# A sparse graph transformer on one core: key products in place, three product buffers, two blocks of states kept in SBUF, output scatters moved and joined

## The chip, the cores and the metric

The kernel runs on one core of a Trainium2 chip. The metric is device time in microseconds (us) of one execution, all four layers included. The engines are named as in the profile: PE (TensorE matmul) and PEld (its weight loads), DVE (VectorE), ACT (ScalarE), POOL (GpSimd) and SP (SyncE, which here only issues transfers).

## The reference

Input `x` holds 16 graphs of 1024 nodes with 128 features, all graphs over the same adjacency matrix `adj` (1024x1024, each entry 1 with probability 1/128). Four layers follow each other: attention, graph attention, attention, attention.

```
def attention_layer(adj, h, ...):            # layers 0, 2, 3
    Q, K, V = h @ Wq, h @ Wk, h @ Wv         # 8 heads of 16
    scores = einsum('bnhd,bmhd->bhnm', Q, K) / sqrt(16)
    scores = where(adj == 0, -inf, scores)
    o = einsum('bhnm,bmhd->bnhd', softmax(scores), V)
    x = layer_norm(h + (o @ Wo + bo), ln1_g, ln1_b)
    y = relu(x @ W1 + b1) @ W2 + b2          # 128 -> 256 -> 128
    return layer_norm(x + y, ln2_g, ln2_b)

def graph_attention_layer(x, adj, ...):      # layer 1
    h = x @ W
    e = leaky_relu((h @ a_src)[:, :, None] + (h @ a_dst)[:, None, :], 0.2)
    att = nan_to_num(softmax(where(adj == 0, -inf, e)))
    return layer_norm(att @ h + x)           # with gain and shift
```

## The kernel before

The function `sparse_path` uses the sparsity of the matrix. Only neighbours enter a softmax, so the kernel gathers the rows of each node's neighbours instead of forming 1024x1024 scores. A second function, `dense_path`, stands behind a flag for inputs that the sparse form can't take; it isn't run here.

**Tiling.** The 16 graphs form two groups (`g`, GR = 2) of eight. The 1024 nodes, reordered by degree, form eight blocks (`t`, T = 8) of 128. A *unit* is one (layer, g, t); `units` lists all 64, and the program goes through them in that order. A unit's state tile, `xs[l, g, t]`, is 128 x (2 halves x 4 graphs x 128) float32, which is 512 KB; the halves `h` go through the tails one by one.

**Tables and gathers.** When a unit of layer l is finished, `project` (L573) writes its new state into the DRAM buffer `kept` (L576, 256 KB for each half) and the projected keys and values into the DRAM table of layer l+1 (L593). All table rows of a group must have been written before that group of the next layer begins. For a unit of the next layer, `loaded` (L881) fetches the state back into a tile of the pool `inputs` (L901, 512 KB), two units ahead; in layer 0 it gathers it from the input (L889). `gathered` (L956) issues indirect transfers from POOL's queue (L971), each bringing one table row to each of the 128 partitions: in an attention layer a row has eight graphs' keys (ROW = 1024 numbers) and values (another 1024), 8 KB. Rows of empty slots are skipped.

**Parts.** A unit's gathered rows are worked off in *parts*, held in `parts`. In an attention layer a unit has five: four with two chunks of rows, and, in fourth place, one shared chunk (`MIX`) of left-over rows. A graph attention unit has three parts, of four, three and two chunks. `es[i]` is the gather buffer of part i; there are four (`EDGES`), so a gather for part i+3 is issued after the last use of part i-1.

**The loop** (L1235) takes one part an iteration. `begun` is the iteration in which the current unit began. In iteration i:

- `products(i)` (L979, L985): DVE multiplies gathered keys with queries into a tile of the pool `prods` (tag `pr`, 8 KB a partition, four buffers). For the shared part POOL does this, in `product_of_shared` (L1000), issued two iterations earlier.
- `summed(i - 2)` (L1067, L1062): PE adds up the weighted values of an earlier part over its rows into `acc`. In attention it takes the first two parts of a unit together. This is what releases a `pr` tile.
- `exponentials(i)` (L1009): DVE sums the products over each head (L1018), ACT takes the exponential (L1022).
- `weighted(i - 1, 0)` (L1036, L1046): DVE multiplies values with the exponentials into the same `pr` tile; in graph attention, which has no key products, the tile is allocated here, and a second call `weighted(i - 1, 2)` takes the part's other two chunks.
- then POOL's work, in this order (L1287): the gathers of part i+3, the shared part's product of part i+2 if that is one, and any output scatter that is in the list `ready`.
- `others()`, three or four times an iteration: steps of the *tails*.

In iteration begun+1 the previous unit is divided by its denominators (L1099, L1102), and its two tails, one for each half, start (`attention_tail` L714, `graph_tail` L766). A tail is a generator: each `yield` is a place where the loop may go on with something else. `PLANS` says by hand which half's tail or which query step runs at each `others()`. The tail of unit u runs while unit u+1 is worked off, and ends in `finish` (L671). In layers 0 to 2 `finish` transposes the state into a tile of the pool `states` and calls `project`. In layer 3 it transposes it back into the tile `outs` (L689) and scatters it to the output rows with an indirect transfer from POOL: a unit's scatter (L702, both halves, 512 KB) goes into `ready`, and only the last unit scatters each half by itself as soon as it is there (L695, 256 KB each, with the row numbers in `halves`). With the plan of layer 3 a unit's `outs` is complete in iteration begun+1 of the unit after the next, so its scatter is issued there, behind the two gathers of part begun+4 and L1000. All scatters write the tensor `out`, and each waits for the one before it to land.

The line that decides on what is issued between gathers:

```
gathered(i - 1 + AHEAD)
product_of_shared(i + 2)
while ready:
    ready.pop(0)()
```

Of the kernel before, what the change touches and what calls it, by code (L numbers as in the profile page):

```python
# [14 lines left out]
F32 = mybir.dt.float32  # L15
# [7 lines left out]
P = 128  # L23
# [21 lines left out]
GR = 2  # L45
# [18 lines left out]
)  # L64
TOP = -(-max(map(max, CAPS)) // 8) * 8
QUADS = TOP // S
MIX = J


# [75 lines left out]
def sparse_path(ctx: ExitStack, tc: tile.TileContext, a: dict, out: bass.AP, flag):  # L145
# [46 lines left out]
    marks = const.tile([P, len(MARK), 32], F32, name="marks")  # L192
    nc.gpsimd.memset(marks, 0.0)
    places = const.tile([P, GR, T], I32, name="places")
    halves = const.tile([P, HF], I32, name="halves")
    bad = const.tile([P, T], F32, name="bad")
    seen = const.tile([P, 2, G * H], F32, name="seen")
    nc.gpsimd.memset(seen, 0.0)
# [37 lines left out]
    def graph(wide):  # L236
# [152 lines left out]
        for g in range(GR):  # L389
            nc.vector.tensor_scalar(  # L390
                places[:, g, :], there, float(GR), float(g), ALU.mult, ALU.add,
            )
        for h in range(HF):
            nc.vector.tensor_scalar(
                halves[:, h : h + 1], there[:, T - 1 :], float(GR * HF), float((GR - 1) * HF + h),
                ALU.mult, ALU.add,
            )
        low = s1.tile([P, T], F32, name="low")
        nc.vector.tensor_tensor(bad, sorted_[:, :, 2], caps[:, :T], ALU.is_gt)
        nc.vector.tensor_scalar(low, sorted_[:, :, 2], 1.0, None, ALU.is_lt)  # L400
# [166 lines left out]
        for l in range(1, len(LAYERS)) for g in range(GR)  # L567
    }
    xs = {}
    srcs = {}  # L570


    def project(l, g, t, h, x, kv=None):  # L573

        if l:
            nc.sync.dma_start(kept[l, g][t, :, h, :], x.rearrange("p g n -> p (g n)"))  # L576
        table = tables[l, g][t * P : (t + 1) * P, :]
        if LAYERS[l][1] is ATTN:
            if kv is None:
                kv = twos.tile([P, 2, GH, D], F32, tag="kv", name="kv")  # L580
            for i in range(0, GH, 2):
                ps = bank([P, 2, 2 * D])
                for k in range(2):
                    nc.tensor.matmul(  # L584
                        ps[:, k, :], x[:, i + k, :], w[LAYERS[l][0], "Wkv"],
                        start=True, stop=True,
                    )
                nc.scalar.copy(  # L588
                    kv[:, :, i : i + 2, :].rearrange("p c g d -> p g c d"),
                    ps.rearrange("p g (c d) -> p g c d", d=D),  # L590
                )
                yield
            nc.sync.dma_start(  # L593
                table.rearrange("p (c x) -> p c x", c=2)[:, :, h * GH * D : (h + 1) * GH * D],
                kv.rearrange("p c g d -> p c (g d)"),
            )
            return
        kv = twos.tile([P, GH * D + GH], F32, tag="kv", name="kv")
        if h == 0:
            srcs[g, t] = const.tile([P, G], F32, name=f"src{g}{t}")  # L600
        for i in range(0, GH, 2):
            ps = bank([P, 2, D + 2])
            for k in range(2):
                nc.tensor.matmul(ps[:, k, :], x[:, i + k, :], wg, start=True, stop=True)
            nc.scalar.copy(
                kv[:, i * D : (i + 2) * D].rearrange("p (g d) -> p g d", d=D), ps[:, :, :D]
            )
            to = GH * D + i
            nc.scalar.copy(
                kv[:, to : to + 2].rearrange("p (g o) -> p g o", o=1), ps[:, :, D : D + 1]  # L610
            )
            at = h * GH + i
            nc.scalar.copy(
                srcs[g, t][:, at : at + 2].rearrange("p (g o) -> p g o", o=1), ps[:, :, D + 1 :]
            )
            yield

        nc.sync.dma_start(table[:, h * GH * D : (h + 1) * GH * D], kv[:, : GH * D])
        nc.sync.dma_start(table[:, ROW + h * GH : ROW + (h + 1) * GH], kv[:, GH * D :])
# [51 lines left out]
    def finish(l, g, t, h, z, gain, shift, dve=False):  # L671
        if l + 1 < len(LAYERS):

            wanted[0] = True
            while held[0]:
                advance(slow)
            wanted[0] = False
            busy[0] += 1
            xn = states.tile([P, GH, P], F32, tag="xT", name="xT")
            turned(z, xn, gain, shift)  # L680
            yield "free"
            yield from project(l + 1, g, t, h, xn)
            busy[0] -= 1
            return
        xn = states.tile([P, GH, P], F32, tag="xT", name="xT")
        turned(z, xn, gain, shift, dve)
        yield
        if h == 0:
            leaving[g, t] = twos.tile([P, HF, GH, D], F32, tag="kv", name="outs")  # L689
        o = leaving[g, t]  # L690
        turned(xn, o[:, h], dve=dve)
        yield
        yield
        if (l, g, t) == units[-1]:
            nc.gpsimd.indirect_dma_start(  # L695
                out=out.rearrange("n (k c) -> (n k) c", k=GR * HF),
                out_offset=bass.IndirectOffsetOnAxis(ap=halves[:, h : h + 1], axis=0),
                in_=o[:, h].rearrange("p g d -> p (g d)"), in_offset=None,
            )
        elif h + 1 == HF:  # L700
            rows = o.rearrange("p h g d -> p (h g d)")
            ready.append(lambda: nc.gpsimd.indirect_dma_start(  # L702
                out=out.rearrange("n (k c) -> (n k) c", k=GR),
                out_offset=bass.IndirectOffsetOnAxis(ap=places[:, g, t : t + 1], axis=0),
                in_=rows, in_offset=None,
            ))

    def hidden():
        return ones_.tile([P, F * GH * P], F32, tag="f1", name="f1")
# [171 lines left out]
    def loaded(u):  # L881
# [1 line left out]
        if u >= len(units):  # L883
            return
        l, g, t = units[u]
        xs[units[u]] = inputs.tile([P, HF, GH, P], F32, tag="x", name="x")
        if l == 0:
            x = xs[units[u]]
            nc.gpsimd.indirect_dma_start(  # L889
# [89 lines left out]
    def products(i):  # L979
        u, (piece,) = parts[i]  # L980
        if i in prs:
            return
        n = len(piece)
        prs[i] = [prods.tile([P, 2, ROW], F32, tag="pr", name="pr")]
        nc.vector.tensor_tensor(  # L985
            prs[i][0][:, :n, :], es[i][:, :n, :ROW],
            of_piece(qs[u], piece),
            ALU.mult,
        )

    def product_of_shared(i):

# [43 lines left out]
    def weighted(i, k0):  # L1036

        u = parts[i][0]
        ex, n = exs_of(i)
        if n <= k0:  # L1040
            return
        m = min(2, n - k0)
        base, d = (ROW, HD) if is_attention(u) else (0, D)
        if not is_attention(u):
            prs.setdefault(i, []).append(prods.tile([P, 2, ROW], F32, tag="pr", name="pr"))
        nc.vector.tensor_tensor(  # L1046
            prs[i][k0 // 2][:, :m, :].rearrange("p k (a d) -> p k a d", d=d),
            es[i][:, k0 : k0 + m, base : base + ROW].rearrange("p k (a d) -> p k a d", d=d),
            ex[:, k0 : k0 + m, :]
            .rearrange("p k (a o) -> p k a o", o=1)  # L1050
            .to_broadcast([P, m, ROW // d, d]),
            ALU.mult,
        )
# [135 lines left out]
    with tc.manual_schedule():  # L1189
# [33 lines left out]
                        advance(slow)  # L1223
                        break
        scratch.close()
        prods = ctx.enter_context(tc.tile_pool(name="prods", bufs=4))
        smalls = ctx.enter_context(tc.tile_pool(name="smalls", bufs=3))
        nc.gpsimd.memset(wide[3], 0.0)
        gathered(AHEAD - 1)
# [5 lines left out]
        for i in range(len(parts) + 2):  # L1235
# [46 lines left out]
            if 0 < i <= len(parts):  # L1282
# [3 lines left out]
                    weighted(i - 1, 2)  # L1286
                gathered(i - 1 + AHEAD)  # L1287
                product_of_shared(i + 2)
                while ready:
                    ready.pop(0)()  # L1290
                for _ in sizes:
                    pass
# [472 lines left out]
```

## Time and profile before

| | |
|---|---|
| time, median of 3 runs | 2123.89 us (2122.29 to 2125.0) |
| profiled execution, its own time | 2126.89 us |
| its span | 2125.0 us |
| PE busy | 1972.9 us (93%) |
| DVE busy | 1806.1 us (85%) |
| ACT busy | 1519.5 us (72%) |
| POOL busy | 1182.4 us (56%) |
| moved by DMA | 636.10 MB, mean 299 GB/s |
| of it POOL's queue (gathers, scatters) | 485.08 MB, 64.3% of 16 engines |
| of it SP's queue (tables, `kept`, loads) | 148.57 MB, 21.3% of 16 engines |

The span runs from the first to the last instruction. Layers follow each other without a gap: DVE divides the last unit of layer 0 at 682.8 us, of layer 1 at 993.4, of layer 2 at 1531.9 and of layer 3 at 2082.0. A matmul's busy time is modelled, so a busy PE isn't PE at its peak. In a timeline a line begins with the start and the duration in us, then come the engine, the line of the kernel, the operation, the tile written and the tiles read, and in brackets how long the engine was idle before it and whose event ended the idle time. That attribution is inferred: where an instruction waits for several things, it names the one whose event came last.

### The profile page before, as it was taken

To read this page: it belongs to the slowest core of one execution; us is meant where nothing else is said; L and a number is where in the kernel's file an instruction comes from. 1 tells how busy PE (TensorE), PEld (TensorE's weight loads), DVE (VectorE), ACT (ScalarE), POOL (GpSimd) and SP (SyncE) were. 2 spreads that over 40 slices of the span, in tenths; PEclk is the share of its full clock that TensorE was granted. 3 is DMA by queue.
4 is the path that set the end of the run, shared out by engine and by line. 5 is a ranking of instruction groups with operands and counts; after the bars stand their busy time and mean duration, and the time that the engine had idled before them with its cause. 6 is when DMAs were issued, how large, how long until landed. Compare 5 with 4: busy or idle time off the path is not lost.

```text
span 2125.0 us, 37303 instructions
## 1 busy us (share of the span) xinstructions
PE 1972.9 (93%) x13444; PEld 1244.8 (59%) x13444; DVE 1806.1 (85%) x1315; ACT 1519.5 (72%) x5051; POOL 1182.4 (56%) x747
## 2 busy tenths in 40 slices
PE   7689999999999999998899999999999999999986
PEld 6455665656666555554466665666656565565554
DVE  6977989999997577677899999999998898989892
ACT  3347878878786555555587887878888777777763
POOL 4344555556555488784454555555566565656550
PEclk8789999999999999999999999999999999999998
DMA  8987888889888799998899999999988878698860
GB/s 275 340 302 260 319 302 303 315 285 316 318 309 292 233 355 356 328 357 315 304 326 328 328 337 316 326 325 338 333 314 281 301 262 305 238 314 282 298 217 22
DMA packets 164800, 636.10 MB, mean 299 GB/s; under 512 B 34664, under 2 KB 37480, under 8 KB 116110
## 3 DMA queue, kind: packets, MB, share of 16 engines
q0 software_dynamic: 88720, 485.08, 64.3%
q1 hardware_dynamic: 75888, 148.57, 21.3%
q8 instruction: 108, 1.77, 0.3%
q14 instruction: 84, 0.69, 0.1%
HBM read 581.08 MB, written 92.34 MB: 317 GB/s over the span
## 4 chain that ended last, share of the span: by engine, by line
PE 49%; DVE 15%; DMA 11%; issue 9%; ACT 6%; POOL 2%; POOLq 0%; DVEq 0%; SPq 0%; ACTq 0%
PE acc L1062 13%; DMA e<-table,idx 10%; PE ps L655 5%; PE yps L755 5%; PE ps L741 5%; DVE pr L985 5%; DVE pr L1046 5%; PE ps L584 4%; DVE sc L1018 4%; PE ps L935 3%; PE yps L730 2%; PE yps L731 2%; PE yps L759 2%; PE ps L926 2%; POOL e L971 2%
## 5 line engine op out<-in xcount | busy, mean ns | idle before, releaser
L971 POOL DMA_INDIRECT e<-table,idx x576 | 877.4, 1523 | 763.2 <-DVE pr L1046 512.4
L1046 DVE TENSOR_TENSOR pr<-e,ex 128x2048 f32<-128x2048 f32 x272 | 617.7, 2280 | 76.9 <-ACT ex L1022 38.8
L985 DVE TENSOR_TENSOR pr<-e,qr 128x2048 f32<-128x2048 f32 x192 | 442.9, 2307 | 75.5 <-DMA e<-table,idx 45.1
L1062 PE MATMUL acc<-pr,marks 128*32 128x512 f32 x2200 | 437.2, 608 | 33.1 <-DVE pr L1046 19.9
L1018 DVE TENSOR_REDUCE sc<-pr 128x128 f32<-128x2048 f32 x192 | 438.9, 2286 | 6.6
L632 ACT ACTIVATE z<-yps,root 128x128 f32<-128x128 f32 x888 | 315.1, 374 | 148.3 <-PE yps L759 106.7
L755 PE MATMUL yps<-W,f 128*128 128x128 f32 x1520 | 249.7, 282 | 7.4 <-ACT f L750 5.5
L648 ACT ACTIVATE z<-yps,rstd 128x128 f32<-128x128 f32 x888 | 252.9, 370 | 3.5
L1062 PEld LDWEIGHTS acc<-pr,marks 128*32 128x32 f32 x2200 | 94.3, 110 | 266.6 <-issue 200.5
L755 PEld LDWEIGHTS yps<-W,f 128*128 128x128 f32 x1520 | 203.5, 191 | 63.0 <-ACT f L750 34.0
L584 PE MATMUL ps<-Wkv,xT 128*128 128x256 f32 x768 | 200.7, 407 | 17.4 <-ACT xT L663 8.3
L938 ACT COPY qr<-ps 128x512 f32<-128x512 f32 x384 | 204.5, 600 | 14.5 <-PE ps L935 12.9
L588 ACT COPY kv<-ps 128x512 f32<-128x512 f32 x176 | 102.7, 588 | 140.7 <-PE ps L584 121.0
L741 PE MATMUL ps<-x,W 128*128 128x512 f32 x384 | 187.2, 611 | 1.2 <-issue 0.9
L632 ACT ACTIVATION_READ_ACCUMULATOR z<-yps,root 128x1 f32 x888 | 188.1, 212 | 0.0
L584 PEld LDWEIGHTS ps<-Wkv,xT 128*128 128x128 f32 x768 | 146.5, 201 | 61.9 <-issue 14.9
L655 PE MATMUL ps<-ident,z 128*128 128x128 f32 x896 | 159.3, 290 | 23.2 <-ACT z L648 13.7
L1000 POOL TENSOR_TENSOR qx<-e,qx 128x1024 f32<-128x1024 f32 x48 | 148.4, 3092 | 57.8 <-DMA e<-table,idx 17.5
L935 PE MATMUL ps<-q,rep 32*128 32x512 f32 x768 | 151.6, 646 | 9.4 <-ACT q L930 7.4
L750 ACT ACTIVATE f<-ps,b 128x512 f32<-128x512 f32 x190 | 127.6, 694 | 44.7 <-PE ps L741 43.9
L730 PE MATMUL yps<-Wo,oT 128*128 128x128 f32 x768 | 155.2, 284 | 1.9 <-ACT oT L661 1.8
L655 PEld LDWEIGHTS ps<-ident,z 128*128 128x128 f32 x896 | 109.0, 143 | 79.6 <-ACT z L648 29.2
(178 smaller groups left out, 2851.0 us busy)
## 6 DMA issues: line engine op xcount, KB each, us to landing
table<-kv SPq DMA_DIRECT2D x88, 512.0 KB
kept<-xT SPq DMA_DIRECT2D x96, 256.0 KB
x<-kept SPq DMA_DIRECT2D x48, 512.0 KB
qx<-qr SPq DMA_DIRECT2D x54, 256.0 KB
e<-table,idx POOLq DMA_INDIRECT x576
table<-kv SPq DMA_DIRECT2D x32, 256.0 KB
qx<-qr SPq DMA_DIRECT2D x48, 128.0 KB
qx<-qr SPq DMA_DIRECT2D x12, 384.0 KB
```

The source lines that it names most:

```text
L584: nc.tensor.matmul(ps[:, k, :], x[:, i + k, :], w[LAYERS[l][0], "Wkv"], start=True, stop=True,)
L632: nc.scalar.activation(z[:, i, :], y[:, i, :], AF.Square, scale=D**-0.5, bias=root, accum_out=total[:, i : i + 1],)
L648: nc.scalar.activation(z[:, i, :], y[:, i, :], AF.Copy, scale=rstd[:, i : i + 1])
L655: nc.tensor.transpose(ps[:, i, :], z[:, i, :], ident)
L741: nc.tensor.matmul(ps, p["W1"][:, f * P : (f + 1) * P], x1.rearrange("p g n -> p (g n)"), start=True, stop=True,)
L755: nc.tensor.matmul(ps[:, i, :], f1[:, f, i * P : (i + 1) * P], p["W2"][:, f, :], start=(f == 0), stop=False,)
L935: nc.tensor.matmul(ps, rep_of(j), q[32 * j : 32 * j + 32], start=True, stop=True)
L971: nc.gpsimd.indirect_dma_start(out=es[i][:, k, :], out_offset=None, in_=tables[l, g][:, :], in_offset=bass.IndirectOffsetOnAxis(ap=idx[:, ...
L985: nc.vector.tensor_tensor(prs[i][0][:, :n, :], es[i][:, :n, :ROW], of_piece(qs[u], piece), ALU.mult,)
L1018: nc.vector.tensor_reduce(sc[:, :n, :], prs[i][0][:, :n, :].rearrange("p k (a d) -> p k a d", d=HD), mybir.AxisListType.X, ALU.add,)
L1046: nc.vector.tensor_tensor(prs[i][k0 // 2][:, :m, :].rearrange("p k (a d) -> p k a d", d=d), es[i][:, k0 : k0 + m, base : base + ROW].rearr ...
L1062: nc.tensor.matmul(outs[32 * j : 32 * j + 32], marks[:, mark, :], rhss, start=(chunk == mine[0]), stop=(chunk == mine[-1]),)
```

## The change

Four things change.

1. `products` writes the product of keys over the keys in the gather buffer `es[i]` instead of into a `pr` tile. `weighted` now allocates the `pr` tile itself, except for the shared part, whose product stays in POOL's tile `qx`. The pool `prods` has three buffers instead of four.
2. The states of block 3 of both groups, `STAYING = ((0, 3), (1, 3))`, get a tile each in a new pool `stay` (4 KB a partition each, together as much as the buffer taken from `prods`). They are in it from layer 0 on: `finish` writes the new state into it, `project` makes no `kept` write for these blocks, and `loaded` makes no load.
3. Output scatters in `ready` are issued in iteration begun+3 only, not in the first iteration that finds them.
4. The last unit's two halves leave with one scatter of 512 KB when the second is there. `halves` and the two operations that compute it go.

```diff
+STAYING = ((0, 3), (1, 3))
...
-        for h in range(HF):
-            nc.vector.tensor_scalar(
-                halves[:, h : h + 1], there[:, T - 1 :], float(GR * HF), float((GR - 1) * HF + h),
-                ALU.mult, ALU.add,
-            )
...
     def project(l, g, t, h, x, kv=None):
 
-        if l:
+        if l and (g, t) not in STAYING:
             nc.sync.dma_start(kept[l, g][t, :, h, :], x.rearrange("p g n -> p (g n)"))
...
-            xn = states.tile([P, GH, P], F32, tag="xT", name="xT")
+            if (g, t) in STAYING:
+                xn = staying[g, t][:, h]
+            else:
+                xn = states.tile([P, GH, P], F32, tag="xT", name="xT")
             turned(z, xn, gain, shift)
...
-        if (l, g, t) == units[-1]:
-            nc.gpsimd.indirect_dma_start(
-                out=out.rearrange("n (k c) -> (n k) c", k=GR * HF),
-                out_offset=bass.IndirectOffsetOnAxis(ap=halves[:, h : h + 1], axis=0),
-                in_=o[:, h].rearrange("p g d -> p (g d)"), in_offset=None,
-            )
-        elif h + 1 == HF:
+        if h + 1 == HF:
             rows = o.rearrange("p h g d -> p (h g d)")
-            ready.append(lambda: nc.gpsimd.indirect_dma_start(
+            issue = (lambda: nc.gpsimd.indirect_dma_start(
                 out=out.rearrange("n (k c) -> (n k) c", k=GR),
                 out_offset=bass.IndirectOffsetOnAxis(ap=places[:, g, t : t + 1], axis=0),
                 in_=rows, in_offset=None,
             ))
+            if (l, g, t) == units[-1]:
+                issue()
+            else:
+                ready.append(issue)
...
-        xs[units[u]] = inputs.tile([P, HF, GH, P], F32, tag="x", name="x")
+        if (g, t) in STAYING:
+            if l == 0:
+                staying[g, t] = stay.tile([P, HF, GH, P], F32, name=f"stays{g}{t}")
+            xs[units[u]] = staying[g, t]
+            if l:
+                return
+        else:
+            xs[units[u]] = inputs.tile([P, HF, GH, P], F32, tag="x", name="x")
...
-        prs[i] = [prods.tile([P, 2, ROW], F32, tag="pr", name="pr")]
-        nc.vector.tensor_tensor(
-            prs[i][0][:, :n, :], es[i][:, :n, :ROW],
-            of_piece(qs[u], piece),
-            ALU.mult,
-        )
+        own = es[i][:, :, :ROW]
+        prs[i] = [own]
+        nc.vector.tensor_tensor(own[:, :n, :], own[:, :n, :], of_piece(qs[u], piece), ALU.mult)
...
         if not is_attention(u):
             prs.setdefault(i, []).append(prods.tile([P, 2, ROW], F32, tag="pr", name="pr"))
+        elif (MIX, 0) not in parts[i][1][0]:
+            prs[i] = [prods.tile([P, 2, ROW], F32, tag="pr", name="pr")]
...
-        prods = ctx.enter_context(tc.tile_pool(name="prods", bufs=4))
+        stay = ctx.enter_context(tc.tile_pool(name="stay", bufs=1))
+        prods = ctx.enter_context(tc.tile_pool(name="prods", bufs=3))
...
-                while ready:
+                while ready and i == begun + 3:
                     ready.pop(0)()
```

More of the change, by code (lines that the diff above doesn't have):

```diff
@@ L194, in sparse_path @@
     places = const.tile([P, GR, T], I32, name="places")
-    halves = const.tile([P, HF], I32, name="halves")
     bad = const.tile([P, T], F32, name="bad")
@@ L569, in sparse_path @@
     xs = {}
+    staying = {}
     srcs = {}
     def project(l, g, t, h, x, kv=None):
-        if l:
+        if l and (g, t) not in STAYING:
             nc.sync.dma_start(kept[l, g][t, :, h, :], x.rearrange("p g n -> p (g n)"))
```

## The prediction

> **What bounds the kernel now.** I read the busy time by stretches first, then what VectorE (DVE) waited for in layer 3, then the timelines of one unit each of layers 2 and 3, then the last microseconds. A unit is one group of graphs and one block of 128 nodes; 16 make a layer. The stretches, with columns as in the header line:
>
> ```profile
> core 0: us, PE busy (x) PEld busy (x) DVE busy (x) ACT busy (x) POOL busy (x), PEclk, DMA share, GB/s
> 648.00:966.00 318.00, 294.02 (x2136) 178.13 (x2136) 219.06 (x270) 183.74 (x726) 229.53 (x166) 0.97 0.92 324
> 966.00:1565.00 599.00, 574.06 (x3828) 363.62 (x3826) 556.60 (x308) 468.32 (x1506) 316.94 (x193) 0.99 0.94 324
> 1565.00:2052.00 487.00, 467.99 (x3010) 282.97 (x3008) 433.47 (x239) 371.39 (x1208) 292.04 (x167) 0.99 0.82 286
> ```
>
> Layer 1 (first row) has DVE at 69% and the DMA engines at 92%: it lives on bytes. Layer 2 (second) has DVE at 93% and DMA at 94%. Layer 3 (third) moves least, 286 GB/s, and yet DVE has 54 us of idle time. PE's share is high in all three, but matmul ends are modelled, so I don't read a bound from it. What DVE waited for between 1634 and 2052 us (line, releaser, total, times, longest):
>
> ```profile
> DVE pr L985 <- DMA e<-table,idx: 31.9, 9, 4.1
> DVE pr L985 <- PE ps L741: 11.8, 3, 4.5
> ```
>
> Twelve waits, one per unit, 43.7 us in all, each before the unit's first key product. Their sizes are alike (3.1 to 4.5 us), so I put the three with PE's name to the same gather: L741 has nothing that L985 reads. With a 1.8 us wait in the unit before, that makes 45.5 us in 13 units. A unit's DVE work is 34.85 us (its period near 1930 us) less 3.75, or 31.1 us. Why is that gather late? First POOL, then DVE, in one unit of layer 3:
>
> ```profile
> 1917.17 2.60 POOL L1000 TENSOR_TENSOR qx<-e,qx 128x1024 f32<-128x1024 f32 x1 [1.14 <-issue]
> 1919.93 3.06 POOL L702 DMA_INDIRECT out<-outs,places  x1 [0.15 <-issue]
> 1923.30 2.99 POOL L971 DMA_INDIRECT e<-table,idx  x1 [0.30 <-ACT z L648]
> 1926.59 1.87 POOL L971 DMA_INDIRECT e<-table,idx  x1 [0.31 <-issue]
> ...
> 1919.79 2.28 DVE L1046 TENSOR_TENSOR pr<-e,ex 128x2048 f32<-128x2048 f32 x1
> 1934.80 2.29 DVE L985 TENSOR_TENSOR pr<-e,qr 128x2048 f32<-128x2048 f32 x1 [3.75 <-DMA e<-table,idx]
> ```
>
> The buffer is free when L1046 ends at 1922.07; POOL is in the output scatter until 1922.99. The two gathers then need until 1928.46 to be issued, and DVE starts 6.3 us after that. The same place in layer 2, where no scatter stands there:
>
> ```profile
> 1242.45 1.03 POOL L971 DMA_INDIRECT e<-table,idx  x1 [2.57 <-DMA kept<-xT]
> 1243.78 2.59 POOL L971 DMA_INDIRECT e<-table,idx  x1 [0.30 <-issue]
> ...
> 1239.89 2.28 DVE L1046 TENSOR_TENSOR pr<-e,ex 128x2048 f32<-128x2048 f32 x1
> 1251.44 2.29 DVE L985 TENSOR_TENSOR pr<-e,qr 128x2048 f32<-128x2048 f32 x1 [0.28 <-ACT qr L938]
> ```
>
> Buffer free at 1242.17, second gather issued by 1246.37 (4.20 us later), DVE on its way 5.1 us after that, and then not for the gather's sake. The end:
>
> ```profile
> 2113.41 0.69 DVE L657 COPY outs<-ps 128x512 f32<-128x512 f32 x1 [0.84 <-PE ps L655]
> 2113.76 0.99 POOL L695 DMA_INDIRECT out<-outs,halves  x1 [26.47 <-ACT outs L661]
> 2117.98 0.97 POOL L695 DMA_INDIRECT out<-outs,halves  x1 [3.23 <-DMA out<-outs,halves]
> ```
>
> The second half's data are ready at 2114.10, but its scatter waits for the first one to land, since both write `out`.
>
> **What the Trainium skill says.** "SBUF — State Buffer", section "Who interferes with whom", has DVE and GpSimd share a port pair; it infers that a `tensor_tensor` takes only its read side and leaves the writing of descriptors alone. The trace disagrees in effect: gather issues take 0.99 us beside a DVE reduction and up to 2.99 beside a two-input product, ending about 0.9 us after it. So a POOL step put just before a product costs more than its own time. "DMA: Bandwidth & Descriptors", section "Issuing engines are not separate DMA queues", says transfers of SP and POOL run on the same 16 engines; so bytes saved on SP's queue can help POOL's gathers. The 0.92 and 0.94 shares agree that the engines are nearly full. "SBUF — State Buffer", section "A bandwidth-pool intuition that's wrong (but worth ruling out)", puts HBM at about 358 GB/s per core; the page's slices of layer 1 show 355 to 357.
>
> **The change, part by part.**
>
> *The scatters of layer 3* move from iteration begun+1 to begun+3. Removed from before the critical gather: 0.92 us of POOL (1922.99 less 1922.07), and the detour into the next product: the second gather is issued 4.20 us after the buffer comes free, as in layer 2, so at 1926.27 and not 1928.46, 2.2 us earlier. The scatter's 512 KB no longer run ahead of it: 5.1 us to DVE's start where there were 6.3, another 1.2. Together 3.4 of the 3.75 us. I leave 0.7 us per unit, and 0.5 for what is late next: POOL's L1000, which may slide into a DVE product when units come faster (layer 2 shows L1046 at 3.75 and 4.42 us instead of 2.28 beside it). 45.5 less 13 x 1.2 is **-30 us**. Bounds: -12 (only 13 x 0.92) and -43 (all of it). In its new place the scatter is issued after the gathers of part begun+6, where POOL next waits for the shared piece's buffer. Behind it stand two gathers, issued by 1934.51 now; 3.06 us of scatter makes 1937.6, landing 6.3 later at 1943.9; their product starts at 1950.1, or 1946.7 with the wait gone. So 2.8 us of cover; without it 3 us a unit come back. DVE at 31.1 us a unit is then the bound; ACT with 371 of 487 us is not.
>
> *The last unit's two scatters become one.* It can start 0.25 us after 2114.10, so 2114.35 for 2117.98: 3.6 us earlier. It carries 512 KB for 256: at the page's mean of 299 GB/s that is 0.9 us more. **-2.75 us**; bounds -1.5 and -3.6.
>
> *Two blocks stay in SBUF.* Gone are 12 of 96 `kept` writes of 256 KB and 6 of 48 loads of 512 KB: 6.3 MB of 636. At 324 GB/s that is 19.4 us of full DMA, the ceiling; the floor is 0 where DVE covers it. By layer, in units of 512 KB: 2 in layer 0 (DMA 86%, DVE has the work: 0), 4 in layer 1 (1.5 us each; I take -5), 4 in layer 2 (1.6 each; -4), 2 in layer 3 (-0.5). **-9.5 us.** On SP's queue 18 issues of 0.3 to 0.6 us go and none is added. The state is now written by the tail itself into the tile it has read (L731); those reads come several tail steps earlier, so I cost that wait at nothing; uncovered it would be one PE step, under 1 us, 12 times.
>
> *Key products in place, three `pr` buffers.* The 192 products stay at 2307 ns each. The trace has no key product in place; L627, which writes over its input, and L642, which doesn't, both take 0.69 us at 128x512, so I take zero (bounds -1 and +5). The products no longer wait for a `pr` buffer; layer 0 has five such waits with PE as releaser, 3.3 us together: -1. The weighted products now do. In attention the tightest reuse is that of part 4 by the next unit's third: PE sums it by 1943.6, the product starts at 1957.96, 14 us of slack. In layer 1 the second tile of part B reuses the first of part A, summed in the same iteration: PE needs 787.02 to 788.94, the product starts about 789.4. Slack 0.4 us, and the same in nearly all layer 1 units; in the first PE comes about 4 us late. **+2 us** (0 to +8), since DMA, not DVE, paces that layer. With the -1, +1.
>
> *Two 128x1 operations for `halves` go*: -0.3 us, like L388's 0.135 us each.
>
> Sum: -30 - 2.75 - 9.5 + 1 - 0.3 = -41.5. The profiled execution took 2126.9 us (span 2125.0); less 41.5 is 2085.4. The median of the three runs shown, 2123.9, lies 3.0 below it, so **2082 us**.
>
> **Rivals.** *The wait stays, since bytes set it.* If the critical gather is slow because the DMA engines are busy, only 0.92 us of 3.5 go: -12 instead of -30, and 2100 us. For it: landing takes 6.3 us in layer 3 against 1 us of issue. Against it: layer 2 moves more and lands in 5.1.
>
> *The third buffer is missed* (this ends slower). Layer 1's second weighted product waits for PE's sums each unit. It holds up its gathers, and these are on the path there (POOL 72% busy, mostly behind DVE). All the rest is worth 43.5 us, so it decides from 43.5/16 = 2.7 us per unit on. At the first unit's 4.2 us it is 67 us, and 2147 us. For it: slack is only 0.4 us. Against it: in 12 of the 15 units that I looked at PE starts those sums within 0.2 us of the end of DVE's L1102, so the two stay in step.
>
> *Bytes count in full:* -19 for -9.5, and all 45.5 us gone: 2057.
>
> *The change doesn't do what it says:* were `kept` writes still made, only 9.5 us would be missing: 2092.
>
> **How the numbers follow.** My forecast (2070 to 2093) 0.58; the bytes rival and partial forms of it (2093 to 2112) 0.17; everything counting (below 2070) 0.13; third buffer or slower products, ending within 0.2% or slower, 0.12. Some 0.2% (4 us) is what a measurement of this kernel can tell from no change. Of the 0.12, 0.03 is within it and 0.09 above. The range 2060 to 2110 leaves out about 0.2.
>
> **What would show it.** Right: the wait before L985 in layer 3 falls from about 3.6 to below 1 us, its period from 34.8 to about 32.4, the scatter follows two gathers; layer 1 shortens by some 3 us net; one scatter ends the program; 630 MB moved. Wrong: 3 us waits at L985 without a scatter ahead, L1046 waiting for PE's `acc` in every layer 1 unit, or L985 slower than 2.31 us.

## The result, and the profile after

| | before | after |
|---|---|---|
| median of six runs, us | 2124.31 (2122.29 to 2125.0) | 2101.75 (2096.53 to 2106.11) |
| profiled execution, us | 2126.89 | 2098.17 |
| its span, us | 2125.0 | 2096.3 |
| moved by DMA, MB | 636.10 | 629.82 |

The ratio is 0.9898 with an interval of 0.9881 to 0.9916: 21.7 us faster, 17.8 to 25.3. The forecast was 2082 us in 2060 to 2110: right in direction and inside the range, but only half of the 41.5 us came, and the time lies in the band (2093 to 2112) that the prediction gave to its bytes rival at 0.17. The profiled execution gained 28.7 us. Cut at DVE's division of each layer's last unit, this lies as follows:

| us | before | after | difference | forecast |
|---|---|---|---|---|
| layer 0 | 682.8 | 683.2 | +0.4 | -1.3 |
| layer 1 | 310.6 | 308.0 | -2.6 | -3 |
| layer 2 | 538.5 | 533.6 | -4.9 | -4 |
| layer 3 | 550.2 | 532.8 | -17.4 | -30.5 |
| after the last division | 43.0 | 38.7 | -4.3 | -2.75 |

The busy time by stretches of the changed kernel follows. As before, the columns are the stretch, its length, the busy time of PE, PEld, DVE, ACT and POOL (with instructions), the granted clock, the DMA share and GB/s:

```profile
648.00:966.00 318.00, 295.31 (x2162) 178.35 (x2158) 223.24 (x274) 185.19 (x730) 225.50 (x167) 0.98 0.93 322
966.00:1560.00 594.00, 574.59 (x3829) 365.58 (x3822) 554.33 (x308) 467.06 (x1504) 313.34 (x193) 0.99 0.94 321
1560.00:2030.00 470.00, 448.36 (x3014) 276.60 (x3014) 439.82 (x239) 370.03 (x1211) 267.35 (x169) 1.00 0.85 295
```

In layers 1 and 2 nothing clear has changed in these columns: 6.3 MB are gone, yet the DMA share is what it was. Layer 3 is denser: its DVE is at 94% and was at 89%.

What DVE waited for in layer 3 (1594 to 2026 us: line, releaser, total, times, longest):

```profile
DVE e L990 <- DMA e<-table,idx: 12.2, 12, 2.4
DVE sc L1019 <- POOL qx L1001: 4.5, 2, 2.3
DVE both L1102 <- PE ps L1065: 3.1, 1, 3.1
DVE both L1102 <- PE ps L651: 3.0, 1, 3.0
```

L990 is the key product (L985 before). Its waits for gathers, with those put down to issue, fell from 45.4 us in 13 units (the layer's third to fifteenth) to 13.5. New is L1019 waiting for POOL's product of the shared part (L1001), and the wait for denominators (L1102) has doubled. One unit, first POOL, then DVE:

```profile
1836.71 1.02 POOL L975 DMA_INDIRECT e<-table,idx  x1 [2.57 <-DVE pr L1049]
1838.04 2.59 POOL L975 DMA_INDIRECT e<-table,idx  x1 [0.30 <-ACT qr L942]
...
1845.04 1.27 POOL L695 DMA_INDIRECT out<-outs,places  x1 [0.30 <-issue]
1846.62 2.11 POOL L975 DMA_INDIRECT e<-table,idx  x1 [0.30 <-issue]
1849.04 0.99 POOL L975 DMA_INDIRECT e<-table,idx  x1 [0.31 <-issue]
...
1845.55 2.29 DVE L990 TENSOR_TENSOR e<-e,qr 128x2048 f32<-128x2048 f32 x1
```

The two gathers at the top are the critical ones, those of a unit's first key product, for which DVE waited before. No scatter stands ahead of them, they take 1.02 and 2.59 us as in layer 2 of before, and the product (last line) has no bracket: it did not wait. The scatter has moved behind them and takes 1.27 us where it took 3.06. But two more gathers stand right behind it. For the later unit whose scatter was issued at 1977.66:

```profile
1977.66 1.27 POOL L695 DMA_INDIRECT out<-outs,places  x1 [0.30 <-issue]
1979.24 1.89 POOL L975 DMA_INDIRECT e<-table,idx  x1 [0.30 <-issue]
1981.44 0.99 POOL L975 DMA_INDIRECT e<-table,idx  x1 [0.31 <-issue]
...
1995.94 2.29 DVE L990 TENSOR_TENSOR e<-e,qr 128x2048 f32<-128x2048 f32 x1 [2.36 <-DMA e<-table,idx]
```

The last line is the product of just these two gathers. They were issued by 1982.43, and it had to wait for them until 1995.94, 13.5 us later. Sorted by the product's place in the unit, the waits are now 3.1 us in all before the critical product, 3.2 before the one whose gathers are issued just ahead of the scatter, and 7.2 (five of 13 units) before the one whose gathers are issued behind it. The last two were zero before.

Where POOL's product meets DVE, POOL first and then DVE:

```profile
1931.94 4.32 POOL L1001 TENSOR_TENSOR qx<-e,qx 128x1024 f32<-128x1024 f32 x1 [3.94 <-DMA e<-table,idx]
...
1931.74 2.28 DVE L1049 TENSOR_TENSOR pr<-e,ex 128x2048 f32<-128x2048 f32 x1
1936.29 1.22 DVE L1019 TENSOR_REDUCE sc<-qx 128x64 f32<-128x1024 f32 x1 [2.27 <-POOL qx L1001]
```

L1001 waited 3.94 us for a gather, so it fell beside a weighted product, took 4.32 us (mean of the page: 2.86), and DVE then waited 2.27 us for it. In layer 3 L1001 waited 29.3 us for gathers, ten times; before, 2.3 us, once. Such waits of DVE and stretched DVE products together went from 1.0 to 9.5 us in the 13 units.

The end of the program, the copy of the second half and the one scatter:

```profile
2087.97 0.69 DVE L653 COPY outs<-ps 128x512 f32<-128x512 f32 x1 [1.56 <-PE ps L651]
2089.43 0.98 POOL L695 DMA_INDIRECT out<-outs,places  x1 [26.57 <-DVE flag L1347]
```

The data are ready at 2088.66 and the span ends at 2096.3, 7.64 us later; before it was 10.9 (2114.10 to 2125.0). And the page's group of key products, with its line of all transfers:

```profile
L990 DVE TENSOR_TENSOR e<-e,qr 128x2048 f32<-128x2048 f32 x192 | 445.9, 2322 | 39.7 <-DMA e<-table,idx 20.4
DMA packets 162193, 629.82 MB, mean 300 GB/s; under 512 B 34360, under 2 KB 37176, under 8 KB 113502
```

2322 ns a product in place against 2307, and the bytes are those of 12 `kept` writes and 6 loads less. The prediction had called a product slower than 2.31 us a sign of being wrong, but the form isn't slower: without the few products over 2.4 us (6 before, 9 here) the mean is 2.28 us in both.

### The profile page after: what moved, and what is told of

Its sections match the earlier page's. It is cut to its first block, busy times and chain, and to the rows that moved or that the text cites. A ratio compares the mean times of both kernels' runs of the same rounds, so it can differ in the third digit from the quotient of the medians.

```text
span 2096.3 us, 37309 instructions
## 1 busy us (share of the span) xinstructions
PE 1948.6 (93%) x13444; PEld 1236.5 (59%) x13444; DVE 1808.5 (86%) x1313; ACT 1515.9 (72%) x5051; POOL 1143.2 (55%) x746
## 2 busy tenths in 40 slices
DMA packets 162193, 629.82 MB, mean 300 GB/s; under 512 B 34360, under 2 KB 37176, under 8 KB 113502
## 3 DMA queue, kind: packets, MB, share of 16 engines
q0 software_dynamic: 88704, 485.08, 65.8%
## 4 chain that ended last, share of the span: by engine, by line
PE 69%; ACT 11%; DVE 7%; DMA 6%; issue 6%; POOL 2%; SPq 0%; POOLq 0%; DVEq 0%; ACTq 0%
PE acc L1065 17%; PE ps L580 8%; PE yps L752 7%; PE ps L651 7%; PE ps L738 7%; PE ps L939 4%; DMA e<-table,idx 4%; PE yps L728 3%; PE yps L756 3%; PE yps L727 3%; DVE pr L1049 3%; PE ps L930 3%; ACT z L628 3%; POOL e L975 2%; ACT qr L942 2%
## 5 line engine op out<-in xcount | busy, mean ns | idle before, releaser
L975 POOL DMA_INDIRECT e<-table,idx x576 | 860.2, 1493 | 751.7 <-DVE pr L1049 506.9
L1049 DVE TENSOR_TENSOR pr<-e,ex 128x2048 f32<-128x2048 f32 x272 | 615.6, 2272 | 101.2 <-ACT ex L1023 51.3
L990 DVE TENSOR_TENSOR e<-e,qr 128x2048 f32<-128x2048 f32 x192 | 445.9, 2322 | 39.7 <-DMA e<-table,idx 20.4
L1019 DVE TENSOR_REDUCE sc<-e 128x128 f32<-128x2048 f32 x192 | 438.9, 2286 | 6.6
L580 PE MATMUL ps<-Wkv,xT 128*128 128x256 f32 x704 | 183.8, 407 | 15.4 <-ACT xT L657 8.5
L1001 POOL TENSOR_TENSOR qx<-e,qx 128x1024 f32<-128x1024 f32 x48 | 137.4, 2862 | 81.2 <-DMA e<-table,idx 48.8
L651 PE MATMUL ps<-ident,z 128*128 128x128 f32 x896 | 153.5, 286 | 21.2 <-ACT z L644 12.0
L580 PEld LDWEIGHTS ps<-Wkv,xT 128*128 128x128 f32 x704 | 134.5, 201 | 56.0 <-ACT xT L657 12.8
L939 PE MATMUL ps<-q,rep 32*128 32x512 f32 x768 | 140.8, 640 | 9.0 <-ACT q L934 7.9
```

Of the source, the lines that this page charges most:

```text
L580: nc.tensor.matmul(ps[:, k, :], x[:, i + k, :], w[LAYERS[l][0], "Wkv"], start=True, stop=True,)
L651: nc.tensor.transpose(ps[:, i, :], z[:, i, :], ident)
L975: nc.gpsimd.indirect_dma_start(out=es[i][:, k, :], out_offset=None, in_=tables[l, g][:, :], in_offset=bass.IndirectOffsetOnAxis(ap=idx[:, ...
L990: nc.vector.tensor_tensor(own[:, :n, :], own[:, :n, :], of_piece(qs[u], piece), ALU.mult)
L1019: nc.vector.tensor_reduce(sc[:, :n, :], prs[i][0][:, :n, :].rearrange("p k (a d) -> p k a d", d=HD), mybir.AxisListType.X, ALU.add,)
L1049: nc.vector.tensor_tensor(prs[i][k0 // 2][:, :m, :].rearrange("p k (a d) -> p k a d", d=d), es[i][:, k0 : k0 + m, base : base + ROW].rearr ...
```

## The experiments

Each run beside the kernel before on the same chip. The chip of the last three (double kept writes, begun with the joined scatter, begun+4) ran the kernel before in 2112.75 us, 11 to 12 us less than the other two (2124.73 and 2123.59), so all are compared by their ratio. "Waits" are DVE's gather waits before key products in the 13 units of layer 3, "collisions" are DVE's waits for L1001 and its stretched products there, both from the one traced execution of each kernel. A wait is called critical, ahead or behind by the product that had it: the unit's first, or the one whose gathers are issued just ahead of the scatter at begun+3, or just behind it.

### The move of the scatters alone

Before, with only this edit:

```diff
-                while ready:
+                while ready and i == begun + 3:
                     ready.pop(0)()
```

> The kernel before with one edit: output scatters of layer 3 are issued in iteration begun+3 only. Theory A (the scatter's place before the critical gather made layer 3's waits): the waits before L985 in layer 3 fall from 45.5 to about 13 us as in the changed kernel, and layer 3 gives nearly all of its 17 us, so about 2107 us. Theory B (layer 3 gained from fewer bytes or from the products in place): the waits stay near 40 us, 2120 us or more.

2105.98 us, ratio 0.9907 (0.9885 to 0.9929), so -19.8 us. Layer 3 takes 528.9 us, waits 13.2 (2.8 critical, 4.3 ahead of the scatter, 6.1 behind it), collisions 6.8. The move alone is nearly all of the change, the new waits included.

### What made the critical gather late: bytes or POOL's slot

Two kernels leave the scatter's place as it was before. The first thins its rows:

```diff
-            rows = o.rearrange("p h g d -> p (h g d)")
+            rows = o.rearrange("p h g d -> p (h g d)")[:, :16]
...
-                out=out.rearrange("n (k c) -> (n k) c", k=GR),
-                out_offset=bass.IndirectOffsetOnAxis(ap=places[:, g, t : t + 1], axis=0),
+                out=out.rearrange("n (k c) -> (n k) c", k=GR * 64),
+                out_offset=bass.IndirectOffsetOnAxis(ap=thin[:, g, t : t + 1], axis=0),
```

> The kernel before, scatters in their old place, but each moves only 64 of its 4096 bytes a row (the last unit's two aside), so the output is mostly not written[...]. Theory A, by the prediction's split: the bytes are 1.2 of 3.4 us of a wait, so some 15 us go, the issue stays at about 3 us beside the product, and the waits before L985 stay at 2 to 2.5 us: about 2109 us. Theory B (bytes set the wait): the waits vanish, layer 3 loses 35 us or more: 2090 us or less.

2121.58 us, 0.9981 (0.9967 to 0.9994). Waits 49.1 us, of which 47.9 critical, where before had 45.4. In the trace, a scatter of 64 bytes a row and the gathers behind it, and then the product:

```profile
1919.10 3.07 POOL L707 DMA_INDIRECT out<-outs,thin  x1 [0.17 <-issue]
1922.47 2.97 POOL L976 DMA_INDIRECT e<-table,idx  x1 [0.30 <-DVE sc L1023]
1925.75 1.88 POOL L976 DMA_INDIRECT e<-table,idx  x1 [0.31 <-issue]
...
1934.11 2.29 DVE L990 TENSOR_TENSOR pr<-e,qr 128x2048 f32<-128x2048 f32 x1 [3.90 <-DMA e<-table,idx]
```

3.07 us of issue for 8 KB, where 512 KB took 3.06, and the same gathers and the same wait behind it. The bytes were worth nothing in these waits. The whole run was 4 us shorter (1.3 to 7.0 by the interval), where theory A had 15; its trace doesn't show where.

The second kernel writes the same bytes in the same place, but from SP's queue and not POOL's, into DRAM that is no longer in use:

```diff
-            ready.append(lambda: nc.gpsimd.indirect_dma_start(
-                out=out.rearrange("n (k c) -> (n k) c", k=GR),
-                out_offset=bass.IndirectOffsetOnAxis(ap=places[:, g, t : t + 1], axis=0),
-                in_=rows, in_offset=None,
+            ready.append(lambda: nc.sync.dma_start(
+                kept[1, g][t].rearrange("p h c -> p (h c)"), rows
             ))
```

> The kernel before, but in the old place the same 512 KB of each unit (the last aside) leave by a plain transfer of SP's queue into a DRAM buffer that nobody reads then, so the output is mostly not written and POOL has no scatter to issue. Theory A: POOL's slot is free, the second gather is issued 2.2 us earlier and only the bytes' 1.2 us stay: waits of about 1.5 us, about 2098 us. Theory B: the bytes are all there, so the waits stay at 3 us or more: 2117 us or more.

2097.66 us, 0.9875 (0.9853 to 0.9896). Waits 10.3 us (6.8 critical), layer 3 526.1 us. Taking the scatter off POOL's queue takes most of the critical wait away (45.4 to 6.8 us) though the bytes are still moved. Both kernels together settle it: the wait was the place in POOL's queue.

### The scatter in another place

The changed kernel, with the scatter in iteration begun. As `outs` is complete only in begun+1, this is the begun of the next unit, later in time than begun+3:

```diff
-                while ready and i == begun + 3:
+                while ready and i == begun:
```

> The changed kernel, with scatters issued in iteration begun (behind the shared part's gather, where POOL stands idle for 3.9 us) and not in begun+3 (ahead of two gathers). Theory C (what layer 3 still lacks is that the scatter holds up the gathers that POOL's product L1001 waits for, so that this product runs into DVE's): L1001 starts earlier, the 9.5 us of DVE time lost to it in layer 3 fall below 4 us, and layer 3 is 6 to 12 us shorter than in the changed kernel: about 2093 us. Theory D (the bytes only move on and delay another gather, or PE sets the pace now): within 3 us of the changed kernel, 2099 to 2105 us.

2088.51 us, 0.9839 (0.9815 to 0.9862): faster than both kernels. Layer 3 519.9 us. But collisions are 8.2 us where theory C wanted under 4; what went were the gather waits, 13.5 to 5.1. C had about the right time for a wrong reason. POOL in one unit:

```profile
1912.40 2.80 POOL L975 DMA_INDIRECT e<-table,idx  x1 [2.63 <-DVE pr L1049]
1915.50 1.02 POOL L695 DMA_INDIRECT out<-outs,places  x1 [0.30 <-issue]
1919.12 1.01 POOL L975 DMA_INDIRECT e<-table,idx  x1 [2.60 <-DVE pr L1049]
```

Between the gathers at 1912.40 and 1919.12 POOL has 3.9 us in which it would only wait for a buffer that DVE still reads. The scatter fits in it, is issued beside a reduction in 1.02 us, and the next gather still waits 2.60 us for DVE afterwards. Nothing is behind it that could have gone earlier.

The changed kernel with all output scatters but the last unit's left out gives the price of the place:

```diff
             else:
-                ready.append(issue)
+                pass
```

> The changed kernel without any output scatter but the last unit's, so the output is mostly not written. It shows what a scatter in iteration begun+3 still costs. Theory C (it holds up gathers): layer 3 some 12 us shorter, as with the scatter in iteration begun or a little more, about 2088 us. Theory D (other waits set layer 3): 2096 us or more.

2090.36 us, 0.9833 (0.9804 to 0.9862). Layer 3 521.1 us, waits 8.4 (7.1 critical), collisions 9.6. So the scatters at begun+3 cost 11 us by the medians (2101.75 less 2090.36) and 14 by the ratios, whose intervals don't overlap; at begun they cost nothing that can be seen. The collisions stay without any scatter: they came with the faster units.

One iteration later than begun+3, behind the gathers that waited:

```diff
-                while ready and i == begun + 3:
+                while ready and i == begun + 4:
```

> The changed kernel with scatters in iteration begun+4: behind the two gathers that begun+3 puts them ahead of, but with their bytes still ahead of the shared part's gather. Theory I (the scatter's time on POOL delays those two gathers, and through them the shared part's): as with iteration begun, 2086 to 2093 us. Theory J (its 512 KB ahead of the shared part's gather make POOL's product late): as the changed kernel, 2099 to 2105 us.

2083.66 us, 0.9859 (0.9838 to 0.9879), which is 2094 us where before takes 2124.31: between the two theories. The product whose gathers stood behind the scatter has no wait left (7.2 to 0.0), waits in all are 2.9. The same view of DVE's waits in layer 3:

```profile
DVE sc L1019 <- POOL qx L1001: 4.5, 2, 2.3
DVE e L990 <- DMA e<-table,idx: 2.9, 5, 1.0
```

But collisions are 16.0 us, and L1001 waits 30.9 us for gathers (22.8 with the scatter at begun). Layer 3 took 525.8 us, where begun+3 had 532.8 and begun 519.9 (and 518.7 in the last kernel below, on the same chip as this one). So both theories were right in part: the wait behind the scatter goes, and about half of the gain is lost where the scatter now stands.

The wait went, but not for the reason that theory I gave. The two gathers need the buffer that L1049 frees when it has read `qx`. Here is that instruction and then the gathers, with no scatter between; below it is the same L1049 in the changed kernel, where the scatter shown above (1977.66) is issued between:

```profile
1960.38 1.21 DVE L1049 TENSOR_TENSOR qx<-e,ex 128x1024 f32<-128x1024 f32 x1
1962.33 2.33 POOL L975 DMA_INDIRECT e<-table,idx  x1 [1.43 <-issue]
1964.96 0.99 POOL L975 DMA_INDIRECT e<-table,idx  x1 [0.30 <-issue]
```

```profile
1976.83 1.22 DVE L1049 TENSOR_TENSOR qx<-e,ex 128x1024 f32<-128x1024 f32 x1
```

Both gathers are out 4.4 us after the buffer is free in either kernel (1965.95 less 1961.59, 1982.43 less 1978.05). Over the 13 units the median is 4.4 us here, 4.6 at begun+3 and 4.7 without any scatter. So POOL's time for the scatter was hidden at begun+3, as the prediction had it; what came later was the landing. In the scatter's old place it was the other way round.

### The products in place with three buffers, alone

The kernel before with the diff's edits to `products`, `weighted` and the pool's size, nothing else:

```diff
...
+        own = es[i][:, :, :ROW]
+        prs[i] = [own]
+        nc.vector.tensor_tensor(own[:, :n, :], own[:, :n, :], of_piece(qs[u], piece), ALU.mult)
...
+        elif (MIX, 0) not in parts[i][1][0]:
+            prs[i] = [prods.tile([P, 2, ROW], F32, tag="pr", name="pr")]
...
-        prods = ctx.enter_context(tc.tile_pool(name="prods", bufs=4))
+        prods = ctx.enter_context(tc.tile_pool(name="prods", bufs=3))
```

> The kernel before with key products in place and three buffers for weighted values; no block stays in SBUF, scatters as before. The move of the scatters alone gave about 19 of the change's 22 us, so the rest adds up to some 3 us where the prediction had 11. Theory E (states kept in SBUF give less than 9.5 us): this kernel is where the prediction put it, within 3 us of before, 2122 to 2127 us. Theory F (the third buffer eats what the states give): 4 to 8 us slower than before, 2129 to 2133 us, with waits of L1046 for PE's acc in layer 1.

2121.42 us, 0.9988 (0.9977 to 0.9999): -2.5 us, with an interval that ends just short of no change. In layer 1 DVE waits for PE as was feared:

```profile
DVE pr L1045 <- PE acc L1061: 15.8, 7, 4.7
```

Before this was 4.8 us in two waits. Still layer 1 takes 306.9 us, not 310.6 or more: waits for exponentials (17.5 to 12.1 us) and for gathers (32.5 to 21.9) shrink by more than that. DVE has slack in this layer, and most of the wait only takes the place of another.

### The joined last scatter, alone

The kernel before with one scatter for the last unit, as in the diff:

```diff
-        if (l, g, t) == units[-1]:
...
-        elif h + 1 == HF:
+        if h + 1 == HF:
...
+            if (l, g, t) == units[-1]:
+                issue()
+            else:
+                ready.append(issue)
```

> The kernel before with the last unit's two scatters joined and nothing else. The prediction had -2.75 us; the changed kernel's trace has 3.3 us less from the second half's copy to the end. So about 2121 us, and if the larger transfer costs what the wait did, 2124 us.

2121.27 us, 0.9989 (0.9977 to 1.0002): -2.3 us by the medians, against -2.75 forecast; the interval just includes no change.

### The states in SBUF

The changed kernel without them:

```diff
-STAYING = ((0, 3), (1, 3))
+STAYING = ()
```

> The changed kernel with STAYING empty, so all blocks write and load their states, 6.3 MB more; products in place, three buffers and scatters as in the changed kernel. Theory E (the bytes are mostly covered by DVE's work): at most 4 us slower than the changed kernel, 2102 to 2106 us. Theory F (the bytes give 9.5 us and the third buffer takes them): about 2111 us.

2101.5 us, 0.9891 (0.9866 to 0.9916), where the changed kernel has 0.9898. Layers 1 and 2 together take 843.9 us against 841.6. By the two intervals the states are worth between -8 and 5 us, so 9.5 is out. The other direction, doubling the bytes in question (every `kept` write is made a second time, into DRAM that nothing reads):

```diff
             nc.sync.dma_start(kept[l, g][t, :, h, :], x.rearrange("p g n -> p (g n)"))
+            nc.sync.dma_start(spare[l, g][t, :, h, :], x.rearrange("p g n -> p (g n)"))
```

> The changed kernel with each of its 84 kept writes made a second time, into a DRAM buffer that nobody reads: 22 MB more, 3.5% of all bytes, mostly in layers 0 to 2. Theory G (bytes of SP's queue have slack beside DVE's work, which is why the states that stay gave nothing): at most 10 us slower than the changed kernel, under 2112 us. Theory H (layers 1 and 2 are at the DMA engines' limit, as the prediction had it): 22 MB at 324 GB/s is 68 us, 2150 us or more.

0.9919 (0.9894 to 0.9944), 2097.07 us there. 651.85 MB are moved, 22 MB more than by the changed kernel, for 0.2% of time, some 4.5 us (-2 to 11 by the two intervals); as full transfer time they would be 68 us. The same stretch of layer 1, first here, then in the changed kernel:

```profile
690.00:960.00 270.00, 251.26 (x1859) 149.41 (x1857) 187.23 (x240) 153.01 (x602) 192.37 (x145) 1.00 0.98 361
```

```profile
690.00:960.00 270.00, 252.06 (x1862) 148.98 (x1862) 186.70 (x241) 153.23 (x617) 197.53 (x145) 0.99 0.93 324
```

PE, DVE and ACT do the same work in the same 270 us, and the DMA engines bring 361 GB/s along, not 324. The chip isn't the reason: layer 1 took 305.5 us here, and 304.7 and 308.4 in the other two kernels traced on it, which moved 340 and 339 GB/s in this stretch. So in layer 1 a share of 0.93 at 324 GB/s was no limit. Layer 2 took 545.6 us here, against 535.9 and 537.4 in those two. If the extra bytes cost anything it is there, but one trace doesn't settle that.

### Two edits on the kernel before

The scatter in iteration begun, and the joined last scatter with the diff shown above; products, buffers and states as before:

```diff
-                while ready:
+                while ready and i == begun:
```

> The kernel before with two edits only: scatters in iteration begun, and the last unit's two joined. No products in place, four buffers, no block stays. If the states and the products in place give nothing, this equals the changed kernel with scatters in iteration begun: 2086 to 2093 us. If they give the 8.5 us of the prediction together, about 2097 us.

2083.29 us, 0.9861 (0.9839 to 0.9882), which is 2095 us where before takes 2124.31. Layer 3 518.7 us, waits 3.4, collisions 8.2, and DVE is busy for 97% of the stretch from 1590 to 2012 us. The ratio lies between the two cases, 5 us above the changed kernel with the scatter at begun (0.9839), and the intervals overlap: this pair alone excludes neither 0 nor the 8.5 us. It does show that two edits reach at least what the whole change did (0.9898).

## Why the prediction was right or wrong

**The critical gather: right, and even short.** With the scatter gone from its front the wait fell to 3.1 us in 13 units, where 9.1 were left in the sum.

**Its split was wrong.** The 3.4 us were put down to 2.2 of issue and 1.2 of bytes. With the thin scatter the critical waits were no shorter (47.9 us for 45.4), so the bytes' share in them was nothing; all was the slot in POOL's queue and what follows from it. It didn't matter for the move, which takes both away. It did for the first rival, which priced the time with bytes as the cause at 2100 us: the number is next to the measured one, the mechanism isn't what happened.

**The cover of 2.8 us was the step that failed.** The working let the scatter push the two gathers behind it 3.06 us back and had them land 6.3 us after their issue, ahead of their product. Both terms were off. The push was 0.2 us by the medians above, as POOL would have waited for the buffer anyway; the landing took up to 13.5 us, as in the timeline above. The text had named this failure ("without it 3 us a unit come back"): it came in five of 13 units behind the scatter, for 7.2 us, and 3.2 more came ahead of it. The 6.3 us had come from a place with less issued ahead. Here four gathers and the scatter are issued within 7.4 us. By the page a gather has some 0.8 MB on average (485.08 MB of POOL's queue less 8.4 of scatters, over 576), so this is about 3.8 MB, or 11 us at the 345 GB/s that the trace has from 1976 to 1996 us: an estimate, near the 13.5 us but short of it. The scatter itself is 0.5 MB of that, 1.5 us. This fits that the same product still waited in four units with the scatter at begun (2.6 us) and in three without scatters (1.3 us), with none right ahead of its gathers: 6.3 us was too short for this place even without the scatter. That it was the scatter's bytes, and not something else in the queue of transfers, is argued from this; no run thinned the scatter at begun+3.

**The collision of L1000 (L1001 after) was mis-sized**: 8.5 us more (1.0 to 9.5) for 6.5. **PE's denominators were not priced**: 3.1 to 6.2 us. Together, in the 13 units: 42.3 us of critical waits gone, 10.4 of other gather waits, 8.5 of collisions and 3.1 of denominators new, 1.4 unplaced; 18.9 us gained of the 30.

**The states in SBUF: -9.5 forecast, nothing found.** The transfers did go (the page counts 84 `kept` writes and 42 loads), so the rival that they would not is out, and the one that their bytes count in full (2057 us) falls with the forecast's half. The failing step is to have read shares of 0.92 and 0.94 as full: the doubled writes took layer 1's from 0.93 to 0.98 and its rate from 324 to 361 GB/s in the same time. A share near 1 doesn't even fix the rate. In the trace of before it is 1.01 from 1260 to 1270 us, at 290 GB/s, and 1.03 from 960 to 970 us, at 421 GB/s (in such short stretches the view's figure can pass 1 a little). The Trainium skill has the better ceiling under "HBM Reference", section "Specifications (TRN2)": a core that streams alone can go well above its share of about 358 GB/s. The 421 GB/s agree, over a short stretch; the 361 GB/s over 270 us lie just above that share. Note that the layers' table hides the error: -7.5 us in layers 1 and 2 for -7 forecast looks right, but that is luck. Without the states they come to -5.2 all the same, and the kernels that have these two layers as before took 843.5 to 849.1 us for them, traced once each, with the trace of before at the slow end. Those with products in place and no state kept took 842.9 and 843.9 us, and those with both 840.6 to 845.5 where no writes were doubled.

**In place, three buffers: near nothing, as forecast.** +1 forecast, -2.5 measured (0 to -5 by the interval, so +1 lies just outside). The waits for PE came in seven places of up to 4.3 us in the change, and the reason given (layer 1 isn't paced by DVE) held, though the doubled writes show that transfers don't pace it either. The rival that put them at 67 us counted each as a loss.

**The last scatter: right.** 3.3 us from the data's readiness to the end, 2.75 forecast, 2.3 by the run with this edit alone.

**The two numbers' bases.** The forecast for a profiled execution was 2085.4 us, and it took 2098.2: 12.8 short, nearly all of it layer 3. The median of the runs lies another 3.6 us above that execution, where the forecast put it 3 below. One execution stands for the median to no better than that. The edits alone, -19.8, -2.3, -2.5 and about 0, sum to -24.6, within the interval of the whole. What stays open is whether the kept states are worth the few microseconds that these runs can't see, and why L1001's gathers land later in the faster units. One slip in the working changes nothing: its bound of -43 for "all of it" should be -45.5, as the rival "bytes count in full" has it.

## What to carry to other kernels

When a transfer is moved out of a queue's critical place, ask two things of the new one. Would the engine that issues it wait there for something else anyway (here, for a buffer that DVE still reads)? And what must land soon after it? At begun+3 the first was so and the second went wrong, so a cover worked out from a landing time must use the load at the new place. A high share of DMA time is no limit until more bytes have been seen to cost time; try doubling them. And try each edit alone: here the move of the scatters did nearly all the work, and the states kept in SBUF did none that could be measured.

## What was not expected of the hardware

The time that POOL needs to issue an indirect transfer did not depend on its bytes: 3.07 us for 64 bytes a row and 3.06 us for 4 KB a row, in the same place. It went with what DVE ran: the same scatter took 1.02 us at begun, beside a reduction, 1.27 at begun+3, at the end of a short product, and 2.95 again in nearly all units at begun+4, beside a product with two inputs. Gathers took 0.99 us beside reductions and up to 3.03 beside such products. At begun+4 the long issue was no loss that the waits before key products show: they were the shortest of all. The Trainium skill's "SBUF — State Buffer", section "Who interferes with whom", infers that such products leave the writing of descriptors alone; the prediction noted that the gathers disagree, and the scatters now do as well.

The DMA engines moved 361 GB/s for 270 us of layer 1 while PE, DVE and ACT kept their pace, and 22 MB more in the whole program cost some 0.2% of the time. At one and the same busy share, about 1, they moved 290 GB/s in one stretch and 421 in another.
